# Two-layer hybrid block on one core: three of sixteen shared experts of the second layer placed between routed experts, the others given out by pieces

## The chip, the core and the metric

The kernel runs on one NeuronCore of a Trainium2 chip. The core has five engines with queues of their own: PE (TensorE, matrix products; the profile lists its weight loads apart, as PEld), DVE (VectorE), ACT (ScalarE), POOL (GpSimd) and SP (SyncE, which here only issues transfers). Each engine takes its instructions in the order in which the program gives them, and a waiting instruction holds what stands behind it on that engine. Transfers between HBM and the on-chip memory are issued from SP, ACT or POOL and are carried out by 16 DMA engines. The time is that of the whole program on the device, in microseconds (us); less is better.

## What is computed

16 sequences of 512 tokens with 256 features, 8192 tokens in all, all float32, pass four steps, each added to its input after a layer norm: attention with rotary positions, a mixture of experts, a linear attention with forget gates, and the same mixture of experts with the same weights again. The change lies in the mixture, which is:

```python
logits = x @ router_w.T                        # 64 experts
probs = softmax(logits)
topk_w, topk_ids = top_k(probs, 8)
topk_w = topk_w / sum(topk_w)
pos = cumsum(onehot)[token, expert] - 1        # place of a token in its expert
valid = pos < 128                              # an expert holds 128 tokens
h = silu(xb @ w_gate) * (xb @ w_up)            # per expert: 128x256 @ 256x192
y = h @ w_down                                 # 128x192 @ 192x256
routed = segment_sum(y[...] * topk_w * valid)  # back to the tokens
shared = silu(x @ ws_gate) * (x @ ws_up) @ ws_down   # every token
return routed + shared
```

The places are counted over all 8192 tokens in order, so an expert takes the first 128 tokens that chose it, and no expert can start before the last token's choice is known.

## The kernel before

Tokens are handled in 16 blocks of 512 (`BLK`), each 4 chunks of 128. `Block.attention` is the first layer, and it works off most of the first mixture's block work between its own steps; `Block.forget_attention` is the linear attention; `Block.routed` finishes a mixture, and with `loads=True` (the second layer) it does all of it. `Part` holds the state of one mixture: pools, weights, and a method for each step of a block. `Block.joined` closes the program.

All the order around the change is written out by hand: inside `tc.manual_schedule` the engines take their instructions in the order in which the code calls the steps.

The second mixture has three stages.

*Block loop* (`for b in range(-4, nb + 1)`, L1266). In one turn it loads block b+4 (`load`), chooses the experts of block b (`choose`, L1573), normalises block b+2 (`normed`), turns block b+1 for PE (`features`), runs the shared expert of block b-3 (`gu`, `silu`; `lag` is 3) and its down product for block b-4 (`down`), takes logits and exponentials of b+1 (`logits`, `likely`, `exps`), counts block b (`count`: turns on PE and a copy on ACT; `added`: a running sum, L1617, carried over from block to block), and takes the moments of block b+3. `choose` divides the exponentials by their sum (L1577 to L1579) before it takes the eight largest (L1587, L1588); the weights are divided by the sum of the eight afterwards. Normalised rows and weights are stored in the table `rows` (`rows<-xn`, `rows<-wt`), counts in the table `counts`, and `counted` reads them back into `cw` with chunks in the partitions (L1506) as soon as they are stored; the last block's counts go from chip memory to `cw` directly (`straight`, L1510, two rows on SP and two on ACT). The shared expert's result y is stored into `routed` on SP (L1691). In turns 2 to 6 one pair of experts' weights is fetched each (`fetch`, four pieces on SP).

*Tail.* `chunks_before` (L1069 to L1073) needs all counts. It copies the chunk totals and forms their running sum on PE. `find` then works out in five pieces which token stands in which place, for two or four experts at a time (`place` advances it), and `gather` fetches the 128 rows of an expert from `rows` (L1133, an indirect DMA on POOL). Between these calls stand the shared experts of the last two blocks and the last three down products.

*Routed experts* (`for e in range(done - 2, E)`). In turn e the kernel gathers expert e+6, advances a lookup, turns the rows of e+2 (`turned`), multiplies e+1 by gate and up (`widened`, L1163), multiplies e by down (`narrowed`, L1187), scales it on ACT into `ye` (L1195) and adds it to the tokens' rows by an indirect DMA on POOL (L1198). Even experts add into the output, odd ones into `routed`, so two accumulators take turns, and an addition waits for the one before into the same accumulator. Weights come in pairs of experts into 11 slots, fetched piece by piece on SP.

At the end `joined` adds `routed` to the output in eight DMAs on POOL (L1381).

Before the stages, `begin` (L1438) loads the router and the shared expert's weights on ACT's queue and stores zeros into the rows behind the last token.

Of the kernel before, what the change touches and what calls it, by code (L numbers as in the profile page):

```python
# [26 lines left out]
E = 64  # L27
# [10 lines left out]
class Block:  # L38
# [131 lines left out]
    def attention(self, x, x1, wqkv, wo, rope, part, later):  # L170
# [14 lines left out]
        with ExitStack() as c:  # L185
# [271 lines left out]
            def each(s):  # L457

                n, i = divmod(s, CB)
                yield groups, n, weighted, i  # L460
                yield groups, n + 2, largest, i
                b, at = divmod(s, steps)

                now = [
                    (self.nblk, b + far, work, *args)
                    for work, far, *args in dense[at]
                    if b + far < z - 2 or work not in expert
                ]
                if i == 0:
                    yield groups, n - 1, summed  # L470
                if i == 1:
                    yield groups, n + 3, turn, kTs, H, "kT"
                    yield from now[0:1]
                    yield groups, n - 1, heads
                    yield groups, n + 1, row
                    now = now[1:]
                if i == 2:
                    yield groups, n + 3, turn, qTs, 0, "qT"
                yield from now
# [542 lines left out]
    def routed(self, part, loads=False):  # L1022
# [9 lines left out]
        with ExitStack() as c:  # L1032
# [6 lines left out]
            if loads:  # L1039
                part.look_up("right")  # L1040
                part.slots(5, "right")
            else:
                part.slots(4, "right")
# [81 lines left out]
            accs = (x, y)  # L1125
# [56 lines left out]
            def narrowed(e):  # L1182
                wd = ws[e // 2][1]
                he = hidden[e % len(hidden)]
                py = bank()
                for m in range(2):
                    nc.tensor.matmul(  # L1187
                        py[:, 0:D],
                        lhsT=he[:, m, :],
                        rhs=wd[:, e % 2, m, :],  # L1190
                        start=(m == 0),
                        stop=(m == 1),
                    )
                ye = p8.tile([P, D], F32, name="ye")
                nc.scalar.activation(  # L1195
                    ye, py[:, 0:D], AF.Copy, scale=xes.pop(e)[:, D + e : D + e + 1]
                )
                nc.gpsimd.indirect_dma_start(  # L1198
                    out=accs[e % 2],
                    out_offset=bass.IndirectOffsetOnAxis(ap=token[:, e : e + 1], axis=0),  # L1200
                    in_=ye,
                    in_offset=None,
                    compute_op=ALU.add,
                )
# [5 lines left out]
            with tc.manual_schedule(  # L1210
# [8 lines left out]
                nb, lag, ahead = self.nblk, 3, 6  # L1219
# [33 lines left out]
                def counts(b):  # L1253
                    part.added(b, stored=b < nb - 1)
                    (part.counted if b < nb - 1 else part.straight)(b)

# [8 lines left out]
                if loads:  # L1265
                    for b in range(-4, nb + 1):  # L1266
# [6 lines left out]
                        run(b - lag, nb, gu)  # L1273
                        run(b - lag, nb, silu)
# [3 lines left out]
                        run(b, nb, counts)  # L1278
                        run(b - 1 - lag, nb, down)
                        run(b + 1, nb, part.exps)  # L1280
                        run(b + 3, nb, lambda b: part.moments(b, xs[b]))
                        if 2 <= b < 7:
                            fetch(b - 2)
                        if b == nb:
                            chunks_before()
                            place(0, 3)

                    begun, done, z = 5, 0, nb - 1
# [3 lines left out]
                    part.gu(z - 1, 0)  # L1292
                    place(2, 1)
                    part.gu(z - 1, 1)
                    place(2, 1)
                    gather_to(3)
                    silu(z - 1)
                    part.down(z - 2, 0)
                    part.down(z - 2, 2)
                    place(4, 3)  # L1300
                    part.gu(z, 0)
                    place(4, 1)
                    part.gu(z, 1)
                    place(4, 1)
                    gather_to(5)
                    silu(z)
                    down(z - 1)
                    down(z)
# [43 lines left out]
                part.own.close()  # L1352
                part.slots(part.pairs - len(part.slot), "left")

                rest = [(n, piece) for n in range(begun, E // 2) for piece in range(4)]
                due, last = len(rest), E - 10
                for e in range(done - 2, E):
                    if e + ahead > 5:
                        run(e + ahead, E, gather_to)
# [4 lines left out]
                    run(e, E, narrowed)  # L1364
                    while rest and (due - len(rest)) * last < due * (e + 1):
                        n, piece = rest[0]
                        if e < 2 * (n - part.pairs) + 3:
                            break
                        if piece == 0:
                            held(n)  # L1370
                        part.fetch(*rest.pop(0))
# [28 lines left out]
class Part:  # L1400
# [6 lines left out]
    def __init__(self, ctx, k, x, y, weights, room, pairs, side):  # L1407
        rw, self.w_gate, self.w_up, self.w_down, ws_gu, ws_down = weights
        self.ctx, self.pairs, self.slot, self.ws = ctx, pairs, [], {}
        self.k, self.nc, self.x, self.y, self.room = k, k.nc, x, y, room  # L1410
# [23 lines left out]
        self.end = 0.0  # L1434
# [3 lines left out]
    def begin(self, queue):  # L1438
        rw, ws_gu, ws_down = self.shared_weights
        nc, T, w = self.nc, self.k.T, self.pools[1]  # L1440
        self.rw_sb = w.tile([P, KD, E], F32, name="rw_sb")
        queue.dma_start(out=self.rw_sb, in_=rw.rearrange("(k p) f -> p k f", p=P))
# [13 lines left out]
        for i in range(self.room["hT"]):  # L1456
            hT = w.tile([P, 2, BLK], F32, name=f"hT{i}")
            nc.gpsimd.memset(hT[FT:P, 1, :], 0.0)
            self.hidden.append(hT)
        for z in (self.rows, self.x, self.y):  # L1460
            queue.dma_start(out=z[T : T + P, :], in_=self.k.zeros[:, 0 : z.shape[1]])

# [47 lines left out]
    def straight(self, b):  # L1510

        for i in range(CB):
            at, queue = b * CB + i, (self.nc.sync, self.nc.scalar)[i % 2]
            queue.dma_start(out=self.cw[at : at + 1], in_=self.cum[:, ts(i, P)])
# [58 lines left out]
    def choose(self, b, piece):  # L1573
        nc, small, pr = self.nc, self.k.small, self.prs[b]
        if piece == 0:
            sm = small.tile([P, CB], F32, name="sm")
            nc.vector.tensor_reduce(sm, pr, AX.X, ALU.add)  # L1577
            nc.vector.reciprocal(sm, sm)
            nc.vector.tensor_tensor(  # L1579
                pr, pr, sm.unsqueeze(2).to_broadcast([P, CB, E]), ALU.mult  # L1580
            )
# [62 lines left out]

    def silu(self, b, piece):
        if piece == 0:
            self.hTs[b] = self.hidden[b % len(self.hidden)]
# [7 lines left out]
    def gate(self, b):  # L1655
# [3 lines left out]
        self.hTs[b] = self.hidden[b % len(self.hidden)]  # L1659
# [15 lines left out]
    def down(self, b, i, pool=None):  # L1675
# [3 lines left out]
        py = self.bank()  # L1679
        for k in range(2):  # L1680
            for m in range(2):
                nc.tensor.matmul(  # L1682
# [6 lines left out]
        nc.scalar.copy(self.ys[b][:, i : i + 2, :], py.rearrange("p (c d) -> p c d", c=2))  # L1689
        if i > 0:  # L1690
            nc.sync.dma_start(  # L1691
                out=self.y[ts(b, BLK), :].rearrange("(c p) d -> p c d", p=P),
                in_=self.ys.pop(b),
            )
            del self.hTs[b]
# [3 lines left out]
def hybrid_block_kernel(  # L1699
# [29 lines left out]
    with ExitStack() as c:  # L1729
        part = Part(c, k, attended, routed, moe, ROOM, 13, "left")  # L1730
# [5 lines left out]
    with ExitStack() as c:  # L1736
        part = Part(c, k, out, routed, moe, ROOMY, 11, "left")
# [73 lines left out]
```

## Time and profile before

| | us |
|---|---|
| three runs | 2657.08, 2655.26, 2654.50 (median 2655.26) |
| the profiled execution, its own time | 2656.52 |
| span from its first to its last instruction | 2654.5 |
| mean granted TensorE clock | 0.951 of full speed |

| share of the span | busy us | instructions |
|---|---|---|
| PE | 2430.0 (92%) | 17864 |
| DVE | 1852.8 (70%) | 4677 |
| ACT | 1333.0 (50%) | 2750 |
| POOL | 843.2 (32%) | 835 |

The shares are means over stages of different kinds. The first attention takes the span to 1339 us with PE at 1320 busy; the first mixture's rest ends at about 1609, the linear attention at about 2128, and the second mixture and the closing sum fill the remaining 526 us. A line of the profile names the source line, the engine, the operation, what is written and read, and how often. In the chain of waits each piece is the work that ended last before the next could start; a timeline lists start, length and the idle time before an instruction with what ended it.

### The profile page before, as it was taken

The page shows a single profiled execution, that of the slowest core. Times are in us where ns is not written, and L with a number is a line of the kernel's source. Part 1 is how long each engine was busy: PE and PEld are TensorE (multiplying, and loading weights), DVE is VectorE, ACT ScalarE, POOL GpSimd, SP SyncE. Part 2 cuts the span into 40 slices and gives each one's busy share as a digit, 9 for nine tenths or more (in the row PEclk, how much of TensorE's full clock was granted, in tenths as well). Part 3 has the DMA queues.
Part 4 walks back from the last instruction along what each step waited for, and adds up shares of the span by engine and source line. Part 5 has one row for each costly group of instructions (what it writes and reads, how often), then busy time and mean ns, then how long its engine had stood idle before and what let it go on. Part 6 is the DMA issues. An engine that isn't in the chain of part 4 may idle for free.

```text
span 2654.5 us, 47730 instructions
## 1 busy us (share of the span) xinstructions
PE 2430.0 (92%) x17864; PEld 1512.9 (57%) x17864; DVE 1852.8 (70%) x4677; ACT 1333.0 (50%) x2750; POOL 843.2 (32%) x835
## 2 busy tenths in 40 slices
PE   7999999999999999999988886899999969998881
PEld 3444555455555554555446775577777646667671
DVE  6566777767777766776646664889889869967660
ACT  1566666666666666666542332466566513323330
POOL 3122212222221222112015776423223021127773
PEclk8899999999999999999888998999999969999996
DMA  1000111001110011100157987212111068749987
GB/s 57 1 10 27 35 37 35 14 29 35 37 35 16 27 37 35 37 27 6 57 123 223 235 223 164 80 34 65 49 57 49 25 149 191 169 113 263 245 212 148
DMA packets 210003, 226.47 MB, mean 85 GB/s; under 512 B 34286, under 2 KB 202222, under 8 KB 208750
## 3 DMA queue, kind: packets, MB, share of 16 engines
q1 hardware_dynamic: 180366, 174.43, 22.8%
q0 software_dynamic: 25728, 46.15, 8.8%
q8 instruction: 142, 2.33, 0.4%
q10 hardware_dynamic: 3680, 2.85, 0.3%
q14 instruction: 87, 0.71, 0.1%
HBM read 146.50 MB, written 84.48 MB: 87 GB/s over the span
## 4 chain that ended last, share of the span: by engine, by line
PE 76%; DVE 9%; DMA 9%; issue 2%; POOL 2%; ACT 1%; SPq 0%; ACTq 0%; POOLq 0%; DVEq 0%
PE sc L334 20%; PE sc L384 9%; DMA xe<-rows,token 5%; PE sc L260 4%; PE pb L809 4%; PE sc L1637 3%; PE sc L323 3%; PE sc L841 2%; PE sc L1682 2%; PE sc L1163 2%; PE pb L873 2%; PE sc L407 2%; PE sc L304 2%; PE pb L918 2%; PE pb L734 2%
## 5 line engine op out<-in xcount | busy, mean ns | idle before, releaser
L348 DVE TENSOR_REDUCE mx<-sc 128x1 f32<-128x512 f32 x1024 | 635.0, 682 | 293.8 <-PE sc L334 293.7
L374 ACT ACTIVATE pT<-sc 128x512 f32<-128x512 f32 x1024 | 527.8, 604 | 110.3 <-PE sc L334 110.3
L334 PE MATMUL sc<-qT,kT 17*128 17x512 f32 x2048 | 315.0, 647 | 0.0
L334 PE MATMUL sc<-kT,qT 16*128 16x512 f32 x2048 | 301.5, 609 | 0.3 <-DVE mx L348 0.3
L384 PE MATMUL sc<-pT,v 128*32 128x512 f32 x2048 | 243.7, 618 | 0.0
L104 POOL TENSOR_SCALAR va<-mv 128x4 f32<-128x4 f32 x64 | 14.6, 228 | 700.8 <-DVE mv L98 690.1
L858 DVE SCALAR_TENSOR_TENSOR pT<-sc,of,left 128x256 f32<-128x256 f32 x512 | 205.0, 474 | 20.2 <-PE sc L841 18.9
L334 PEld LDWEIGHTS sc<-kT,qT 16*128 16x128 f32 x2048 | 151.1, 190 | 91.9 <-issue 36.5
L282 POOL TENSOR_TENSOR t<-qk,rope_sb 128x512 f32<-128x512 f32 x62 | 78.6, 1267 | 382.2 <-ACT qk L268 374.6
L334 PEld LDWEIGHTS sc<-qT,kT 17*128 17x128 f32 x2048 | 94.3, 185 | 128.4 <-issue 95.3
L384 PEld LDWEIGHTS sc<-pT,v 128*32 128x32 f32 x2048 | 61.6, 113 | 174.2 <-issue 124.0
L1133 POOL DMA_INDIRECT xe<-rows,token x128 | 128.7, 1006 | 96.9 <-DVE token L1115 39.6
L260 PE MATMUL sc<-wqkv_sb,feat 128*128 128x512 f32 x256 | 124.8, 613 | 0.0
L144 ACT COPY oT<-sc 128x512 f32<-128x512 f32 x64 | 37.4, 585 | 172.7 <-PE sc L384 172.7
L809 PE MATMUL pb<-feat,wqk_sb 128*128 128x512 f32 x256 | 117.7, 593 | 0.0
L1198 POOL DMA_INDIRECT routed<-ye,token x64 | 102.9, 1608 | 41.7 <-DMA routed<-ye,token 9.6
L323 PEld LDWEIGHTS sc<-ident,pad 128*128 128x128 f32 x512 | 55.3, 144 | 104.2 <-ACT pT L374 81.9
L96 DVE BATCH_NORM_STATS2 bn<-x 128x6 f32<-128x256 f32 x256 | 89.1, 411 | 16.8 <-DMA x<-out 13.4
L1597 POOL TENSOR_TENSOR wt<-pr,chosen 128x256 f32<-128x256 f32 x32 | 23.2, 725 | 241.4 <-DVE chosen L1592 217.1
L323 PE MATMUL sc<-ident,pad 128*128 128x128 f32 x512 | 86.8, 293 | 5.1 <-POOL pad L298 2.8
L1637 PE MATMUL sc<-xnT,wsg_sb 128*128 128x512 f32 x192 | 90.9, 600 | 0.0
L290 POOL TENSOR_TENSOR t<-qk,rope_sb 128x256 f32<-128x256 f32 x124 | 90.6, 752 | 0.0
(225 smaller groups left out, 4900.3 us busy)
## 6 DMA issues: line engine op xcount, KB each, us to landing
ws<-in_w_gate SPq DMA_DIRECT2D x64, 384.0 KB
ws<-in_w_up SPq DMA_DIRECT2D x64, 384.0 KB
rows<-xn SPq DMA_DIRECT2D x32, 512.0 KB
routed<-y SPq DMA_DIRECT2D x32, 512.0 KB
ws<-in_w_down SPq DMA_DIRECT2D x64, 256.0 KB
x<-in_x SPq DMA_DIRECT2D x16, 512.0 KB
attended<-x SPq DMA_DIRECT2D x16, 512.0 KB
ws<-in_w_down SPq DMA_DIRECT2D x64, 128.0 KB
```

The source lines that it names most:

```text
L260: nc.tensor.matmul(pq, lhsT=xnTs[b][:, kd, ts(i, P)], rhs=wqkv_sb[:, kd, 0 : 2 * D], start=(kd == 0), stop=(kd == KD - 1),)
L290: eng.tensor_tensor(t2[:, :, lo : lo + HD // 2], qk2[:, :, :, 1 - half], rope_sb[:, i, HD + lo : HD + lo + HD // 2] .unsqueeze(1) .to_broa ...
L323: nc.tensor.transpose(pt[:, ts(i, P)], pads[b % 2][i][:, at : at + 4, :].rearrange("p h d -> p (h d)"), self.ident,)
L334: nc.tensor.matmul(scs[j], lhsT=lhs[at : at + high, ts(i, P)], rhs=rhs[at : at + high, :], start=True, stop=True,)
L348: nc.vector.tensor_reduce(mxs[n][:, j, i : i + 1], sc, AX.X, ALU.max, negate=True)
L374: nc.scalar.activation(pT[:, j, :], sc, AF.Exp, scale=float(HD) ** -0.5)
L384: nc.tensor.matmul(pav[ts(j, HP), :], lhsT=vs[b % 2][:, i, 4 * hg + j, :], rhs=pT[:, j, :], start=(i == 0), stop=(i == CB - 1),)
L809: nc.tensor.matmul(pq, lhsT=wqk_sb[:, kd, ts(m, P)], rhs=xnTs[b][:, kd, :], start=(kd == 0), stop=(kd == KD - 1),)
L858: nc.vector.scalar_tensor_tensor(pTs[n][:, :, ts(s8, HD)], sc[:, :, ts(s8, HD)], of[:, s8 : s8 + 1], here, ALU.mult, ALU.mult,)
L1133: nc.gpsimd.indirect_dma_start(out=xes[e], out_offset=None, in_=rows, in_offset=bass.IndirectOffsetOnAxis(ap=token[:, e : e + 1], axis=0),)
L1198: nc.gpsimd.indirect_dma_start(out=accs[e % 2], out_offset=bass.IndirectOffsetOnAxis(ap=token[:, e : e + 1], axis=0), in_=ye, in_offset=No ...
L1637: self.nc.tensor.matmul(to, lhsT=self.wsg_sb[:, kd, ts(m, P)], rhs=self.xnTs[b][:, kd, :], start=(kd == 0), stop=(kd == KD - 1),)
```

## The change

It does these things:

- `choose` no longer divides by the sum of the exponentials; this holds for both mixtures.
- Blocks 3, 7 and 11 of the second mixture are put off (`put_off`): their shared expert is left out of the block loop, and zeros are stored for them in `begin`. It runs between the routed experts in 24 pieces (`between`), with the shared weights loaded a second time and the normalised rows read back from `rows`; three DMAs on POOL add the results (`paid`).
- The other 13 blocks' shared experts are a list of pieces with costs, 130 units in all, of which each turn of the loop gives out its share up to 110; the last 20 go before and between the lookups.
- Counts are read back one block later (`counted` of b-1), `straight` issues all four rows on ACT, and y is stored on ACT's queue in the second mixture.
- Early weights are fetched as two pieces in every block from 3 on, in place of four in blocks 2 to 6. The second mixture has 9 slots of weights, not 11.
- The accumulators are taken in turn (`next(accs)`) whoever adds.

The core of the diff:

```diff
-            accs = (x, y)
+            accs = itertools.cycle((x, y))
...
-                    out=accs[e % 2],
+                    out=next(accs),
...
                 if loads:
-                    for b in range(-4, nb + 1):
+                    own = [b for b in range(nb) if b not in part.put_off]
...
+                    pieces = []
+                    for n, b in enumerate([*own, None]):
+                        if b is not None:
+                            pieces.append((4, b, first_part, b))
+                        if n > 0:
+                            pieces.append((2, own[n - 1], part.down, own[n - 1], 0))
+                            pieces.append((2, own[n - 1], part.down, own[n - 1], 2))
+                        if b is not None:
+                            pieces.append((2, b, second_part, b))
+                    total, spent = 10 * len(own), 0
...
+                    for b in range(-4, nb):
...
-                        run(b - lag, nb, gu)
-                        run(b - lag, nb, silu)
+                        shares((total - 20) * (b + 1) // nb, b)
...
-                        run(b, nb, counts)
-                        run(b - 1 - lag, nb, down)
+                        run(b, nb, lambda b: part.added(b, stored=b < nb - 1))
+                        if b == nb - 1:
+                            part.straight(b)
+                        run(b - 1, nb - 1, part.counted)
...
-                        if 2 <= b < 7:
-                            fetch(b - 2)
+                        for _ in range(2):
+                            if b >= 3 and early:
+                                part.fetch(*early.pop(0))
+                    shares(total - 10)
+                    chunks_before()
+                    place(0, 3)
+                    shares(total - 8)
                     place(0, 2)
                     gather_to(1)
                     place(2, 3)
+                    shares(total - 6)
+                    place(2, 2)
                     gather_to(3)
...
                 for e in range(done - 2, E):
+                    if open_piece:
+                        next(filler, None)
+                        open_piece = False
...
+                    if e >= 0 and begun_pieces * (E - 14) < all_pieces * (e + 1):
+                        next(filler, None)
+                        open_piece = begun_pieces % 8 > 0
+                        begun_pieces += 1
+                    if part.owed and e >= E - 12 and e % 3 == 0:
+                        part.paid(next(accs))
...
+        for b in self.put_off:
+            for i in range(CB):
+                at = b * BLK + i * P
+                queue.dma_start(out=self.y[at : at + P, :], in_=self.k.zeros[:, 0:D])
...
     def choose(self, b, piece):
         if piece == 0:
-            sm = small.tile([P, CB], F32, name="sm")
-            nc.vector.tensor_reduce(sm, pr, AX.X, ALU.add)
-            nc.vector.reciprocal(sm, sm)
-            nc.vector.tensor_tensor(
-                pr, pr, sm.unsqueeze(2).to_broadcast([P, CB, E]), ALU.mult
-            )
...
+    def between(self, side):
...
+        for b in self.put_off:
+            xn = pool.tile([P, CB, D], F32, name="xn_o")
+            nc.sync.dma_start(
+                out=xn, in_=self.rows[here, 0:D].rearrange("(p c) d -> p c d", c=CB)
+            )
+            yield
+            for kd in range(KD):
+                pt = self.bank()
+                for i in range(CB):
+                    nc.tensor.transpose(
+                        pt[:, ts(i, P)], xn[:, i, ts(kd, P)], self.k.ident
+                    )
+                yield
+                nc.scalar.copy(xnT[:, kd, :], pt)
+                yield
+            for m in (0, 2, 1):
+                gu = self.bank()
+                self.chunk(b, m, gu)
+                yield
...
+            for i in (0, 2):
+                py = self.bank()
+                self.lowered(py, hT, i)
+                yield
+                nc.scalar.copy(y[:, i : i + 2, :], py.rearrange("p (c d) -> p c d", c=2))
+                yield
+
+    def paid(self, to):
+        here, y = self.owed.pop(0)
+        self.nc.gpsimd.dma_start(
+            out=to[here, :].rearrange("(p c) d -> p c d", c=CB), in_=y, accum_op=ALU.add
+        )
...
-        part = Part(c, k, out, routed, moe, ROOMY, 11, "left")
+        part = Part(c, k, out, routed, moe, ROOMY, 9, "left", (3, 7, 11))
```

`chunk` is a gate or up product of a block (two float32 matmuls of 512 columns, which the profile lists as four rows) and `lowered` the down product of half a block (the four matmuls that `down` had before, eight rows). After each matmul piece the copy, tanh or SiLU that reads it stands at the start of the next expert's turn.

## The prediction

> **What bounds the kernel now.** The change reaches almost only the second expert layer, so I read the stretches first (start and end in us, length, busy us with instruction counts of PE, PEld, DVE, ACT and POOL, granted clock, DMA share, GB/s), cut where that layer changes character:
>
> ```profile
> 2142.40:2341.20 198.80, 179.31 (x795) 128.69 (x796) 182.22 (x628) 58.51 (x112) 41.67 (x64) 0.87 0.72 167
> 2341.20:2378.80 37.60, 34.63 (x122) 21.84 (x121) 18.55 (x40) 8.84 (x16) 6.14 (x6) 0.95 0.34 99
> 2378.80:2575.00 196.20, 166.24 (x1119) 146.00 (x1117) 129.33 (x362) 65.08 (x170) 140.77 (x112) 0.97 0.91 243
> 2575.00:2609.30 34.30, 21.93 (x146) 18.66 (x146) 10.94 (x31) 9.09 (x23) 22.53 (x18) 0.92 0.53 84
> 2609.30:2654.50 45.20, 0.00 (x0) 0.00 (x0) 0.00 (x0) 0.00 (x0) 6.80 (x8) 0.50 0.91 186
> ```
>
> The block loop is VectorE's (182.22 of 198.80 busy); the tail up to the first expert is TensorE's (34.63 of 37.60, DMA at 0.34); the experts use PE, POOL and DMA heavily together; the closing sum is DMA alone. The timeline of DVE in the loop shows what a block is made of (start us, us, engine, line):
>
> ```profile
> 2300.93 0.38 DVE L1577 TENSOR_REDUCE sm<-pr 128x4 f32<-128x256 f32 x1
> 2301.34 0.18 DVE L1578 RECIPROCAL sm<-sm 128x4 f32<-128x4 f32 x1
> 2301.55 0.42 DVE L1579 TENSOR_TENSOR pr<-pr,sm 128x256 f32<-128x256 f32 x1
> 2302.01 0.23 DVE L1587 MAX8 top<-pr 128x8 f32<-128x64 f32 x1
> ...
> 2307.11 0.67 DVE L1018 SCALAR_TENSOR_TENSOR th<-th,pb 128x512 f32<-128x512 f32 x1
> ...
> 2309.92 0.42 DVE L1564 TENSOR_REDUCE mx<-pb 128x4 f32<-128x256 f32 x1
> ```
>
> Nothing waits between them: scans (L1617) start at 2298.16 and 2310.72, 12.56 us a block. Normalising is 2302.01 - 2300.93 = 1.08 us of it, a shared expert's SiLU 2309.92 - 2307.11 = 2.81 us.
>
> The chain of waits shows the tail as shared experts (L1637 gate and up, L1682 down):
>
> ```profile
> 2354.29 5.33 PE pb L1637 x8
> 2359.61 0.64 PE pb L1095 x4
> 2360.25 1.91 PE pb L1637 x4
> 2362.17 3.45 PE pb L1682 x16
> 2365.62 3.43 PE pb L1637 x8
> ...
> 2372.05 6.91 PE pb L1682 x32
> ```
>
> So a block costs PE 5.15 (row 2332.67 of the same chain) + 3.46 = 8.6 us. For the experts, POOL's timeline:
>
> ```profile
> 2462.13 1.59 POOL L1198 DMA_INDIRECT routed<-ye,token  x1 [0.30 <-issue]
> 2464.03 0.99 POOL L1133 DMA_INDIRECT xe<-rows,token  x1 [0.30 <-issue]
> 2466.09 1.59 POOL L1198 DMA_INDIRECT out<-ye,token  x1 [1.08 <-DMA out<-ye,token]
> 2467.98 0.99 POOL L1133 DMA_INDIRECT xe<-rows,token  x1 [0.30 <-issue]
> 2469.27 1.59 POOL L1198 DMA_INDIRECT routed<-ye,token  x1 [0.30 <-ACT th L1172]
> ```
>
> A gather and a scatter-add cost 0.99 + 0.30 + 1.59 + 0.30 = 3.18 us, and POOL has little rest: 64 experts took 2596.7 - 2378.8 = 217.9 us, 3.40 each. PE's own need comes from the rows at 2561.67, where the turns of an expert start, and 2564.39, where the next lookup starts: 2.72, plus a quarter of a lookup's 1.09, 2.99 us. POOL leads, PE follows.
>
> **The change, part by part, to the profiled execution** (2656.52 us; span 2654.5, 2.0 around it).
>
> *Loop.* (a) Normalising goes, 16 x 1.08 = -17.3 us, all of it on DVE's path up to the last scan; the ratio of the weights is unchanged by it. (b) Before that scan 13 SiLUs ran; the new budget, 110 of 130 units, holds 12 first and 11 second halves, 11.5: -1.5 x 2.81 = -4.2. (c) Counts are read back a block later, y goes out on ACT's queue. The waits of SP's queue show
>
> ```profile
> SPq L1506 <- DMA counts<-cum: 56.6, 13, 6.7
> ```
>
> (total us, times, longest), with x loads and stores queued behind. But DVE lost only some 5 us to late transfers in the loop (from scan 2162.47 to scan 2339.92 177.5 us; blocks 9.67, 12.56 and the shorter last ones add up to 172.6). The bounds are -5 and +5 (y's issue on ACT, 0.41 us on SP, holds up the copies and tanh behind it when an older transfer is late); I take 0, because weights now come as two pieces in every block from 3 on and keep DMA as full as the 0.84 that I read for 2185 to 2230. (d) begin() gets 12 more stores of zeros, 1.5 MB, on ACT's queue just where the first x loads run; the same row's kind, 1.5 MB of x, took from 2138.3 to about 2145 there, so 0 to +6; +2, since DVE needs the second and third x only 5 and 10 us later. On ACT the first copy is at 2148.24, with 11 us of room against 12 x 0.4 us of issue. (e) The first shared expert starts at block 0 rather than 3. The granted clock was 0.50 until 2182 and 0.70 then 1.00 as L1637 began; 12 matmuls at half clock cost 5.15 more. 0 to +5; I take +2, nearer the lower end because the clock was already 0.70 over the first 3 us of them.
>
> The Trainium skill, "TensorE: Matmul & The Clock Gate", Part 1, says that about 3.4 us of sustained matmuls release the clock. The windows at 2182 to 2188 agree; by the rule (e) would be some 1.7 us, by the row of half clock 5.2.
>
> The Trainium skill, "DMA: Bandwidth & Descriptors", Rules for kernel authors, speaks against (c): other issuing queues share the same 16 engines, and only issue time is saved. By it (c) is 0; if SP's 56.6 us were all on the path it would be far more, which the 172.6 excludes.
>
> Loop: -17.3 - 4.2 + 2 + 2 = -17.5.
>
> *Counts to lookup.* From the last scan to L1069 took 2351.76 - 2339.92 = 11.8 us, because SP issued its two rows (L1514) only at 2347.5. All four on ACT: scan 1.3, issues 2.4 (1.19 for two), landing 3.0 (after 2348.7) to 6.4 (first layer, 1386.1 to 1392.5): 6.7 to 10.1. Ten units on PE beside it (8.6 us, then tanh 0.6 and DVE 1.4) end about 9 after the scan. I take 9: -2.8 (bounds -5, -1.7).
>
> *Tail.* From 2351.76 to 2378.80 is 27.0 us. Now 5 x 1.73 of shared work, lookups 0.68 + 0.64 + 1.09, the first product 0.6, and some 2 for the last tanh and SiLU: 13.6. The other path, tokens 4.0 + issue 1.4 + landing 4.5, is shorter. -13.4 (bounds -16, -9). The first expert starts 33.7 earlier.
>
> *Experts.* Three blocks return: 8 turns 0.87 (L1543 x8 in the chain) + 8.61 = 9.5 each, 28.4 us of PE, spread over experts 0 to 49: PE then needs 2.99 + 0.57 = 3.56 a piece, against 3.40 taken before, so +8; up to 28.4 if POOL loses all of it, 0 if it overlaps wholly. ACT gets 18 copies and tanh of 0.6 and DVE 12 operations of 0.7, in 65 and 129 busy of 196: hidden; without cover 11 and 8. A tanh or SiLU that waits for a piece holds ACT's ye and DVE's xeT behind it, POOL's scatter next. DMA: three xn of 0.5 MB, 0.58 MB of shared weights again, through SP ahead of weight fetches: 2.1 MB at 243 GB/s is 9 us in a stretch with 9% free, hence +1. The weights' two memsets on POOL replace two of six for slots (11 pairs become 9). Three sums of 0.5 MB are turns of the accumulators on POOL at experts 54, 57, 60: joined's rows give 0.85 to issue, 5.65 us per MB, so 1.15 + 2.8 = 4 each if scatters wait, 12; gathers end at 57 and DMA is 0.53 there, so +5. Together +14 (0 to +40).
>
> *Rest.* First layer: two more issues on ACT (0.56 and 0.85) ahead of tanh at 1386.13, in its chain: +1.4. Its removed normalising lies beside PE, at 1320 of 1339 busy, or ends 2 us before the count's turns: 0. Closing sum unchanged.
>
> Sum: -17.5 - 2.8 - 13.4 + 14 + 1.4 = -18.3, span 2636.2, execution 2638.2. The runs' median, 2655.26, is 1.3 below the profiled execution: **2637 us**.
>
> **Rivals.** *Expert stage pays everything* (slower). PE's order and POOL's 3.18 decide: a piece stands before the next turns, ye comes late, and POOL, with 0.22 us of rest an expert, never catches up. 28.4 + 12 = +40 in place of +14: 2663. For: 3.56 is above both 3.18 and 3.40. Against: 6 gathers ahead and 8 buffers of ye, and PE itself waited 27.8 us for xe. It decides from +38 on, 4.0 us an expert. *Loop bound elsewhere*: PE (43.0 of 45 busy from 2185) and DMA 0.84 keep the pace, (a) gains 4 only: 2637 + 13 = 2650. Against: PE's load falls from 11.6 (turns 0.87, logits 1.73, count 0.43, shared 8.6) to 8.9 us a block, DVE's to about 10.5. *All hidden*: PE's pieces fall into its waits, sums behind the last experts, +0: 2623.
>
> **How the numbers follow.** Forecast 0.50, all paid 0.20, loop elsewhere 0.14, all hidden 0.16. 0.2% (5.3 us) is about what a measurement tells from no change: faster than 2650 is the forecast, all hidden and 0.02 of the loop's case, 0.68; 0.12 of that case and 0.01 of all paid are within, 0.13; 0.19 slower. The range: down to -14 on the experts and -5 on transfers with some loss elsewhere, 2616; up to all paid, 2663.
>
> **What would show it.** After: scans 10.5 us apart with SiLU, no L1577 to L1579; last scan near 2322; first expert near 2345; experts 3.5 to 3.6 us each to 50, POOL idle waiting for ye; first joined near 2591. Wrong if DVE idles over 10 us in the loop for L1637 or x, if experts take 3.8 and more, or if scatters wait over 4 us after each sum.

## The result and the profile after

The changed kernel takes 2668.58 us (median of 11 runs, 2661.36 to 2673.47); the kernel before, run on the same chip, takes 2656.5 us (11 runs, 2650.64 to 2663.11). The ratio is 1.0036 with a 95% interval of 1.0024 to 1.0049: about 10 us slower, where 18 us less were forecast, and outside the range. The profiled execution after took 2668.04 us, span 2666.1, at a mean granted clock of 0.946.

Cut at the same marks in both traces (the last addition of the first mixture's experts on POOL; the last scan of the counts; the copy of the chunk totals; the first expert's turns on PE; the first DMA of the closing sum), the spans compare like this, in us:

| stretch | before | after | difference | predicted |
|---|---|---|---|---|
| start to the first mixture's last addition | 1644.9 | 1652.7 | +7.8 | +1.4 |
| from there to the last scan (linear attention, block loop) | 695.0 | 696.2 | +1.2 | -17.5 |
| last scan to the copy of the totals | 11.8 | 15.9 | +4.0 | -2.8 |
| copy of the totals to the first expert | 27.0 | 18.2 | -8.8 | -13.4 |
| experts | 230.5 | 237.6 | +7.1 | +14 |
| closing sum | 45.2 | 45.5 | +0.3 | 0 |

The first mixture's experts end at this mark, 1644.9 before, and not at the 1609 that the section on the time before gives. The first row is mostly scatter between executions: in the traces of the kernels below, whose first layers are nearly alike, this mark lies anywhere from 1641.9 to 1653.3. The second row is the one that counts. A loop that should have become 17.5 us shorter did not become shorter at all.

The stretches of the kernel after (start and end in us, length, busy us with instruction counts of PE, PEld, DVE, ACT and POOL, granted clock, DMA share, GB/s):

```profile
2153.20:2350.20 197.00, 169.47 (x765) 119.84 (x766) 163.39 (x574) 55.64 (x107) 41.73 (x64) 0.89 0.71 174
2350.20:2383.10 32.90, 21.51 (x68) 13.66 (x67) 14.63 (x35) 4.70 (x9) 5.53 (x5) 0.79 0.34 83
2383.10:2578.00 194.90, 186.10 (x1227) 161.75 (x1226) 136.90 (x374) 75.64 (x188) 142.35 (x113) 1.00 0.95 257
2578.00:2620.65 42.65, 22.82 (x146) 20.32 (x146) 10.96 (x31) 9.20 (x24) 27.02 (x20) 0.83 0.65 99
2620.65:2666.10 45.45, 0.00 (x0) 0.00 (x0) 0.00 (x0) 0.00 (x0) 6.83 (x8) 0.50 0.90 185
```

VectorE's work in the loop fell as foreseen, from 182.22 to 163.39 us. But the stretch is still 197 us long, so 17.0 of the 18.8 us that the work lost came back as idle time (33.6 us of it, where the kernel before has 16.6), while PE and the DMA engines are no fuller than before. Something that is none of these three holds the loop. VectorE's timeline shows what it waits for (in brackets the idle time and what ended it):

```profile
2275.45 1.27 DVE L1666 TENSOR_TENSOR_SCAN cum<-cs,cum 64x512 f32<-64x512 f32 x1
2282.07 1.40 DVE L97 BATCH_NORM_STATS2 bn<-x 128x6 f32<-128x256 f32 x4 [5.35 <-DMA x<-out]
...
2290.96 1.27 DVE L1666 TENSOR_TENSOR_SCAN cum<-cs,cum 64x512 f32<-64x512 f32 x1
```

These two scans are 15.5 us apart, and 5.35 of that is a block of x that came late. Up to block 13, blocks without a stall are 10.0 to 11.5 us apart, 10.7 on the mean, close to the predicted 10.5. In the waits of VectorE from 2160 to 2350 (total us, times, longest) x has the first place; the same wait took 3.0 us, once, in the kernel before:

```profile
DVE bn L97 <- DMA x<-out: 14.2, 5, 5.4
DVE mx L1618 <- PE pb L1606: 5.8, 3, 4.8
```

The second line belongs for the most part to the longest interval, 20.8 us before block 11, in which PE stalls too (e9 below). The chain of waits leads from x to its cause:

```profile
2243.86 0.59 ACT y L1733
2244.48 5.15 DMA routed<-y
2249.64 0.37 SPq L1548
...
2255.33 11.14 DMA x<-out
2266.50 1.41 DVE bn L97 x4
...
2277.56 3.47 PE pb L1745 x16
2281.05 0.59 ACT y L1733
2281.67 8.87 DMA routed<-y
2290.55 0.66 SPq L1548
2291.25 4.60 DMA x<-out
2295.88 1.40 DVE bn L97 x4
```

Read it upwards: VectorE waits for x, x was late because SP issued it late (and, the first time, because its transfer took 11.14 us, not 4.60), SP stood at a fetch of weights (L1548), and that fetch waited until a store of y, issued by ScalarE, had landed. The fetch has no data in common with y. SP's own timeline shows the hole:

```profile
2264.05 0.27 SPq L1560 DMA_DIRECT2D cw<-counts  x1
2274.75 0.38 SPq L1548 DMA_DIRECT2D ws<-in_w_gate  x1
2275.18 0.53 SPq L1548 DMA_DIRECT2D ws<-in_w_up  x1
2275.75 0.47 SPq L1062 DMA_DIRECT2D x<-out  x1
```

From 2264.32 to 2274.75 SP issued nothing, 10.4 us, and x is third in the line behind. The store it waited for is this one, in ScalarE's timeline:

```profile
2267.99 0.37 ACTq L1735 DMA_DIRECT2D routed<-y  x1
```

SP had reached the fetch 3.7 us before ScalarE even issued the store; in seven of its eight such waits SP stood before the store was issued. The waits of SP's queue over the loop and the tail (total us, times, longest) add up to 79.6 us of this:

```profile
SPq L1548 <- DMA routed<-y: 62.3, 6, 15.0
...
SPq L1650 <- DMA routed<-y: 8.8, 1, 8.8
SPq L1587 <- DMA routed<-y: 8.5, 1, 8.5
```

In the kernel before, SP's queue waited 0.2 us for y in this stretch, and 67.5 us for its own counts, which are now down to 2.3. One wait took the place of the other, and the new one is longer each time (up to 15.0 in place of 6.7). The records of the trace say why. Each transfer signals its landing by a completion semaphore, and in every trace of this case all transfers issued by SP and ScalarE share one ring of eight such semaphores; POOL's use eight others. The fetch of 2274.75 signals the same semaphore as the store of 2267.99 and waited for it before it was issued, and the seven transfers that SP had issued just before it carry the seven other semaphores. So in this program a transfer that would use a semaphore again waits until the earlier transfer on it has landed, whichever of the two engines issued that, and SP can run at most seven transfers ahead of a store that ScalarE has not issued.

The tail has the same queue in it. Its chain of waits after:

```profile
2348.94 1.29 DVE cum L1666
2350.25 9.06 DMA cw<-cum
2359.33 0.47 ACTq L1568
...
2364.82 0.22 DVE after L1072
...
2365.62 3.71 PE pb L1745 x8
2369.33 1.15 PE pb L1098 x4
2370.48 3.70 PE pb L1745 x8
...
2374.86 0.49 DVE near L1109
...
2378.41 1.16 PE pb L1098 x8
```

ScalarE's four issues of the last counts, in its timeline

```profile
2350.25 9.55 ACTq L1568 DMA_DIRECT2D cw<-cum  x4
```

took 9.5 us in place of the 2.4 that were booked: they start at 2350.25, 2350.84, 2354.45 and 2359.33, and the third and the fourth stood until an earlier transfer on their semaphore had landed. In addition PE, idle meanwhile, came back at half clock: 3.71 us for eight rows of L1745 that take 1.73 at full clock.

### The profile page after: what moved, and what is told of

The parts are those of the page before. It is cut to its first block, busy times and chain, and to the rows that moved or that the text cites. A ratio compares the mean times of both kernels' runs of the same rounds, so it can differ in the third digit from the quotient of the medians.

```text
span 2666.1 us, 47722 instructions
## 1 busy us (share of the span) xinstructions
PE 2435.6 (91%) x17888; PEld 1519.8 (57%) x17888; DVE 1820.6 (68%) x4581; ACT 1337.5 (50%) x2756; POOL 847.9 (32%) x838
## 4 chain that ended last, share of the span: by engine, by line
PE 78%; DVE 8%; DMA 7%; issue 2%; POOL 1%; ACT 1%; SPq 0%; ACTq 0%; POOLq 0%; DVEq 0%
PE sc L335 20%; PE sc L385 9%; PE sc L261 4%; PE pb L811 4%; PE sc L1686 3%; PE sc L324 3%; DMA xe<-rows,token 3%; PE sc L843 2%; PE sc L1745 2%; PE pb L1167 2%; PE pb L875 2%; PE sc L408 2%; PE sc L305 2%; PE pb L920 2%; PE pb L736 2%
## 5 line engine op out<-in xcount | busy, mean ns | idle before, releaser
L1686 PE MATMUL sc<-xnT,wsg_sb 128*128 128x512 f32 x192 | 90.9, 600 | 0.0
```

The lines of the kernel that those rows point to most:

```text
L1686: self.nc.tensor.matmul(to, lhsT=self.wsg_sb[:, kd, ts(m, P)], rhs=self.xnTs[b][:, kd, :], start=(kd == 0), stop=(kd == KD - 1),)
```

## The experiments

All times are medians of several runs against the kernel before on the same chip; differences in per cent and us are taken from the ratios. "After" is the changed kernel; where an edit starts from another version, it says so.

**y stored from SP again (e1).**

```diff
             if loads:
                 part.look_up("right")
                 part.slots(5, "right")
-                part.queue = nc.scalar
```

> The changed kernel with y stored on SP's queue again. In the changed kernel's trace SP's weight fetches, rows stores and x loads waited 80 us for y's stores (62.3 + 8.8 + 8.5), and DVE stood 25.3 us for x. Theory S (a transfer on SP waits for an earlier store that ACT issues late, and everything behind it on SP is late): DVE's wait for x falls below 10 us, first to last scan from 173.9 to some 155 us, the kernel 2668 -> about 2650. Rival D (the DMA engines are full in the loop, whoever issues): the same bytes move, the wait stays near 25 us, the time stays within 4 us of 2668.

2649.32 us, ratio 0.9961 [0.9946, 0.9976]. One line of the change thus costs 0.75%, 20 us, and without it the change is a gain. From the first mixture's last addition to the last scan it takes 680.7 us, 15.5 less than after, the scans are 10.0 to 11.7 us apart but for one (15.6) and the two shorter ones at the end, and neither SP waits for y nor VectorE for x in the loop. Another 2.7 us come from the counts in the tail: last scan to copy 13.2 against 15.9.

**y stored from POOL (e2).**

```diff
-                part.queue = nc.scalar
+                part.queue = nc.gpsimd
```

> The changed kernel with y stored on POOL's queue, neither ACT nor SP. Theory S: SP no longer waits for y at all, DVE's wait for x falls below 8 us, first to last scan some 152 us, the kernel about 2648; POOL has 12 of 15 us free in the loop and pays about 1 us a store. Rival D: as with SP, within 4 us of 2668. If the store's place in the order matters more than its queue, this run gains and the one with SP does not.

2652.63 us, 0.9972 [0.996, 0.9985]; the loop takes 681.9. So it isn't that y must be on SP to be in time. A third queue, outside the ring of semaphores, does nearly as well, and it is ScalarE's queue that does the harm.

**The store on ScalarE alone, put into the kernel before (e11).**

```diff
         if i > 0:
-            nc.sync.dma_start(
+            self.queue.dma_start(
...
-        self.end = 0.0
+        self.end, self.queue = 0.0, k.nc.sync
...
                 part.slots(5, "right")
+                part.queue = nc.scalar
```

> The kernel before, with y of the second mixture stored from ScalarE's queue and nothing else changed. Theory A (transfers issued on SP wait for stores issued on ScalarE, whatever else is done): the profile shows SP waiting some 20 to 80 us for routed<-y in the loop, x later at VectorE than before, last scan 3 to 15 us later counted from the first; ratio 1.002 to 1.006. Rival B (the store on ScalarE costs only together with the counts that are read back a block later, since in the kernel before SP waits for its counts in any case): waits for routed<-y under 15 us, ratio 0.998 to 1.001.

2676.96 us, 1.0067 [1.0043, 1.0091], 17.8 us slower (11 to 24 by the interval): theory A, above the upper end of what it expected. The lines of SP's waits:

```profile
SPq L1621 <- DMA routed<-y: 58.9, 7, 15.4
SPq L1507 <- DMA counts<-cum: 51.5, 15, 7.0
```

Four blocks are 17.0 to 18.9 us apart where the others are 12.6, and VectorE waits 20.8 us for x in the loop, 3.0 before. Here nothing else of the change is present, so the cost needs neither the new order nor the later read-back.

**Only the normalising removed, from the kernel before (e3).**

```diff
-            sm = small.tile([P, CB], F32, name="sm")
-            nc.vector.tensor_reduce(sm, pr, AX.X, ALU.add)
-            nc.vector.reciprocal(sm, sm)
-            nc.vector.tensor_tensor(
-                pr, pr, sm.unsqueeze(2).to_broadcast([P, CB, E]), ALU.mult
-            )
```

> The kernel before, with the three normalising instructions of choose taken out and nothing else. My prediction's term: 16 x 1.08 us on DVE's path in the loop, so 2656 -> about 2639, first to last scan from 177.5 to some 161 us. Rival D: DMA or PE keeps the pace, the loop shortens by 4 us or less and DVE's wait for transfers grows instead, the kernel about 2652.

2656.37 us, 0.9988 [0.9975, 1.0001]: some 3 us of the 17.3, between 0 and 7 us by the interval. Undisturbed blocks are 11.5 apart in place of 12.6, so the edit is worth its 1.1 us in them; but three blocks now take 15.8 to 16.9 where one took 15.6 before, SP waits for its counts 73.5 us, 67.5 before, and VectorE waits for x 14.0 us, 3.0 before. At the new pace SP's queue no longer brought x in time.

**The normalising back in, y on SP (e7, from e1).** The same lines with plus signs.

> The changed kernel with y on SP and the normalising put back. In the kernel before, taking it out gave only some 3 us, because waits for x grew from 3.0 to 13.8 us. If those waits came from counts read back at once and weights in bunches, they are gone here, DVE alone holds the loop, and the 16 x 1.08 = 17 us show: 2649 -> about 2665. If PE or DMA holds the loop even so, it costs under 8 us: below 2657.

2662.8 us, 1.0016 [1.0003, 1.003]; against e1 0.55%, 14.6 us. Eleven of the fifteen intervals between scans grow by 1.1 us. With a queue that keeps up, the same three instructions are worth nearly what was predicted, 14.6 for 17.3; on the kernel before they were worth 3.

**The counts read back in their own block, y on SP (e8, from e1).**

```diff
-                        run(b - 1, nb - 1, part.counted)
+                        run(b, nb - 1, part.counted)
```

> The changed kernel with y on SP and counts read back at once, as in the kernel before. SP waited 67.5 us there for counts to land. If that wait is what made x late, DVE's wait for x comes back (5 to 15 us beside the first) and the kernel is 6 to 15 us above 2649. If bunched weights were the cause, or DVE has room for it, it stays within 3 us of 2649, and the last read-back may gain or lose 2.

2666.32 us, 1.0031 [1.002, 1.0042]; against e1 0.70%, 18.6 us. VectorE waits for x 14.3 us again. SP's queue waits for its counts:

```profile
SPq L1558 <- DMA counts<-cum: 68.7, 15, 7.1
```

So the part of step (c) that was booked at nothing holds a gain of 18.6 us and a loss of 20 us.

**No block put off (e4, from after; e6, from e1).**

```diff
-        part = Part(c, k, out, routed, moe, ROOMY, 9, "left", (3, 7, 11))
+        part = Part(c, k, out, routed, moe, ROOMY, 9, "left", ())
```

> The changed kernel with no block put off: all 16 shared experts by pieces (160 units, 140 of them in the loop), no zeros, no pieces between experts, no three sums; 9 slots stay. By the traces the expert stage took 237.6 us against 230.5, so it should fall back by 7 to about 231; the loop gets 2.5 more shared experts in it, 7 us of DVE, and more waits of SP for y if theory S holds. Both together: between 2664 and 2680. If putting off itself were what costs (my second rival before the run, 28 us and more in the expert stage), it would end below 2655.

> The changed kernel with y on SP and no block put off. Putting off by itself: the expert stage should fall from 238 to some 228 (225.8 was seen with none put off), while the loop gets 2.5 shared experts more, 2.5 x 2.8 = 7 us of DVE, if DVE is what holds the loop. So between 2644 and 2650, near no difference from y on SP alone. If the loop is held by transfers, the three stores of y more cost over 7 and it ends above 2652; if the pieces between the experts cost more than the stage shows, below 2642.

e4: 2671.45 us, 1.0042 [1.0029, 1.0054], no different from after. e6: 2657.72 us, 0.9992 [0.9979, 1.0005], 8 us slower than e1 where 2644 to 2650 was expected: a miss. In the traces e6's loop takes 699.8 us against e1's 680.7, and its experts 229.5 against 238.0. With y on ScalarE the same trade is even: loop 707.0 against 696.2, experts 225.8 against 237.6. So with y on SP putting off pays 8 us here, but more than the 2.5 shared experts in the loop is behind it. Without blocks put off, the budget gives out a second half and a down product of the same block in turns 4, 5, 12 and 13. In just these turns PE waits for VectorE's SiLU, 3.96, 1.03, 5.23 and 1.85 us, and the scans stand 16.2, 13.8, 15.4 and 13.8 us apart where their undisturbed neighbours stand 11.5 or less. This is the stall that e9 takes out of turn 11; how much putting off is worth without it was not run.

**The counts of the block before read back first (e5, from e1).**

```diff
+                        run(b - 1, nb - 1, part.counted)
                         run(b, nb, lambda b: part.added(b, stored=b < nb - 1))
                         if b == nb - 1:
                             part.straight(b)
-                        run(b - 1, nb - 1, part.counted)
```

> The changed kernel with y on SP, and counted of the block before put ahead of the last block's added and straight. With y on SP the lookup waited for the read-back of block 14, which SP could issue only at 2337.33, after the last block's direct rows (5.0 + 6.9 us in the chain). If that order on SP is what is late, the way from the last scan to the copy of the totals falls from 13.2 to 8 to 9 us and the kernel is 4 to 5 us below the one with y on SP (2649). Rival: the direct rows on ACT (2.5 us of issue, 5 of landing) end no earlier than the read-back would: within 2 us of it.

2645.2 us, 0.9948 [0.993, 0.9965]; on the average 0.13% better than e1, 3.5 us where 4 to 5 were expected, with intervals that overlap. The chain of e1 in the tail shows what it aims at: SP issued the read-back of block 14's counts only after the last scan, at 2337.33.

```profile
2332.35 4.97 DMA cw<-cum
...
2337.33 6.85 DMA cw<-counts
...
2344.26 0.23 DVE after L1071
```

In e5 the read-back goes out at 2334.65, before its last scan at 2334.97, and the copy follows 10.0 us after the scan, 13.2 in e1.

**A down product never in the turn of its own second half (e9, from e5).** In e1, e5 and e7 one scan interval stays long, 15.6 to 18.2 us, at block 11. PE's timeline of e1 there:

```profile
2281.78 0.59 PE L1744 MATMUL pb<-wsd_sb,hT 128*128 128x256 f32 x2
2287.39 2.93 PE L1744 MATMUL pb<-wsd_sb,hT 128*128 128x256 f32 x6 [5.01 <-DVE hT L1021]
2290.11 2.45 PE L1605 MATMUL pb<-rw_sb,xnT 128*128 128x64 f32 x16
```

Turn 11 is the only one in which the budget gives out the second half of block 9, the first of block 10 and a down product of block 9. That product needs the SiLU of its own block, which stands behind all of VectorE's other work of this turn, and the next block's logits (L1605) stand behind the product.

```diff
+                        fresh = set()
                         while pieces and spent + pieces[0][0] <= upto and pieces[0][1] <= newest:
-                            cost, _, work, *args = pieces.pop(0)
+                            if newest < nb and pieces[0][2] == part.down and pieces[0][1] in fresh:
+                                break
+                            cost, of, work, *args = pieces.pop(0)
+                            if work is second_part:
+                                fresh.add(of)
```

> The version with y on SP and the counts of the block before read back first (ratio 0.9948) still has one scan interval of 17.1 us at block 11, where the others are 10 to 11.5. Theory: turn 11 is the only one that gives out a second half (block 9) and a down product of the same block, so PE stands waiting for that block's own SiLU, behind everything that VectorE has to do first, and then runs at half clock. With the down product held until turn 12 the interval falls to about 11, the other stages stay, and the time falls by about 5 us: ratio 0.993. Rival: the long interval comes from a late row of x or from the clock alone; then it stays above 15, the ratio is 0.995.

2635.46 us, 0.9916 [0.9893, 0.9939]. The interval at block 11 is 11.5 us. This version is 22 us faster than the kernel before and 1.2% faster than the change as made. Its loop takes 678.5 us, 16.5 less than before, where the prediction has 17.5. The interval shows that the stall is gone; the total doesn't resolve what it was worth, for the interval of the ratio overlaps that of e5, and e10, which keeps the stall (15.65 us), is as fast.

**The last counts on SP and ScalarE in turn (e10, from e5; e12, from e9).**

```diff
-            at = b * CB + i
-            self.nc.scalar.dma_start(out=self.cw[at : at + 1], in_=self.cum[:, ts(i, P)])
+            at, queue = b * CB + i, (self.nc.sync, self.nc.scalar)[i % 2]
+            queue.dma_start(out=self.cw[at : at + 1], in_=self.cum[:, ts(i, P)])
```

> The same version with the last block's four rows of counts on SP and ScalarE in turn again, as before the change, in both mixtures. Theory: in the first mixture ScalarE's two extra issues stand in the chain, some 1.2 to 2 us, which come back; in the second, SP has nothing late in front of its two rows once the counts of the block before are read back first, so last scan to copy of totals stays at 10 us or falls to 9. Ratio 0.994 (from 0.9948). Rival: SP's rows stand behind SP's store of y and its read-back as in the kernel before, the copy of totals comes 11.8 us or more after the last scan, and the ratio is 0.995 to 0.996.

> The down product held until the next turn (ratio 0.9916 by itself) and the last block's counts on SP and ScalarE in turn (0.992 against 0.9948 without, where 0.994 was expected) together: y on SP, the counts of the block before read back first. If the two gains are independent, the ratio is 0.9916 - 0.0028 = 0.989; if the gain of the two queues was only spread between chips, it stays at 0.9905 to 0.992, with the copy of totals 10.4 us after the last scan as in both.

e10: 2638.88 us, 0.992 [0.99, 0.994]; e12: 2636.37 us, 0.9921 [0.9907, 0.9935]. e10 came out below the 0.994 expected, which is the end of its interval, but e12 is no better than e9, so no gain of the two queues can be told: last scan to copy is 10.4 us in e10 and 10.2 in e12, 10.5 in e9. The 1.2 to 2 us that ScalarE's two extra issues should cost in the first mixture are not resolved by these runs.

## Why the prediction was wrong, step by step

**The step that failed is (c)**, the queue of y and the later read-back, put at 0 with bounds of -5 and +5. The store on ScalarE costs 17.8 us alone (e11) and 20 us inside the change (after against e1). Its upper bound was built from y's issue on ScalarE and what is queued behind it there. It was not asked what on SP might wait for y, since no data ties SP's transfers to it, and the rule on issuing queues that the prediction quotes there speaks of bandwidth and issue time, not of such a wait. The other half of (c), the read-back a block later, is not nothing either: e8 has all the rest of the change with y on SP, and its loop takes 696.9 us, no less than the 695.0 before. The prediction took 5 us of late transfers in the kernel before from a sum of 172.6; the undisturbed intervals add up to about 174, which leaves the 3 us for which VectorE waited for x. Either figure said only how well SP's waits were hidden at 12.6 us a block; at 11.5 they lie bare, as e3 shows. So the later read-back is what lets the loop have the gains of (a) and (b) at all, 18.6 us. The forecast's 0 for it was a silent assumption that SP keeps up at the new pace, which the read-back makes true. Of the 18.7 us by which the loop missed its forecast, 15.5 are the store's (after against e1), 2.2 are the stall of block 11 (e1 against e9) and 1.0 is left.

**(a) Normalising, -17.3.** Right in kind: 1.1 us a block in e7 against e1, 14.6 us in all. The forecast treats it as a term that stands by itself, and e3 shows that it doesn't: alone it is worth some 3 us.

**(b), (d), (e) and the rest of the loop.** Taken together with (a) and a harmless (c), the loop was to lose 17.5 us; with y on SP it lost 14.3 (e1) and with the stall of block 11 gone 16.5 (e9). That stall, 5.0 us of PE waiting in e1, was not foreseen: pieces were counted, and which piece stands before which was not followed turn by turn. The zeros (d) can't be seen: the first scan comes 522.3 us after the last addition in after and 522.7 in e4, which stores none. For (d) and (e) together +4 was booked. With the old start of the loop this way takes 517.5 (before), 520.0 (e3) and 520.5 us (e11), with the new one 520.5 (e7) to 524.6 (e9), 522.8 on the mean, so some 3 us are seen. The first shared expert now runs on PE ahead of the first count (5.57 us of L1686 for 12 rows at 2165.32), and with no trace of the zeros these 3 us are probably its; no run tests it alone.

**Counts to lookup, -2.8 with bounds -5 and -1.7; measured +4.0.** The 9 us that were forecast became 15.9. The two things missing are both queues: ScalarE's four issues took 9.5 us, since two of them waited for earlier transfers, and the read-back of block 14 was late. With y on SP and the read-back first it is 10.0 (e5) and 10.5 (e9), a gain of 1.3 to 1.9.

**Tail, -13.4 with bounds -16 and -9; measured -8.8.** 18.2 us in place of 13.6. The first three pieces of PE after the copy ran at half clock, 3.71 + 1.15 + 3.70 where 1.73 + 0.64 + 1.73 had been booked, 4.5 us; and 3.5 us of VectorE's own steps between two lookups (2374.86 to 2378.37) were left out, while the 2 us that were booked for tanh and SiLU, and one of the five pieces of shared work, lay beside other work. Even in e9 the stage takes 16.7.

**Experts, +14; measured +7.1.** The sum was too high, and wrong inside. Three blocks of work on PE were booked at +8, since PE would need 3.56 us an expert against 3.40. But 3.40 is a mean over all 64, with the last thirteen at 2.9. The first 50, where the pieces stand, took 3.63 us each before and 3.56 after. The same kernels without pieces took as long as those with them (3.56 in e4 and in after, 3.62 in e6 and in e1), so no cost of the 28.4 us of PE work can be seen; e5, at 3.72, shows the scatter. The last thirteen took 37.6 us before and 46.2 after (45.2 in e1, 46.1 in e9; 36.9 in e6 and 35.7 in e4, which have no sums). That is 8 to 10 us for the three sums, booked at 5 and bounded by 12. POOL's timeline after shows two of them:

```profile
2596.98 1.55 POOL L1813 DMA_DIRECT2D routed<-y_o  x1
2600.62 1.60 POOL L1202 DMA_INDIRECT out<-ye,token  x1 [2.09 <-ACT wc L1158]
...
2608.21 0.92 POOL L1813 DMA_DIRECT2D routed<-y_o  x1 [0.69 <-DMA routed<-ye,token]
2610.51 1.61 POOL L1202 DMA_INDIRECT out<-ye,token  x1 [1.38 <-DMA out<-ye,token]
2614.41 1.57 POOL L1202 DMA_INDIRECT routed<-ye,token  x1 [2.30 <-DMA out<-ye,token]
```

A sum takes POOL up to 1.6 us, not the 1.15 booked, and additions that followed each other 1.9 to 2.7 us apart at the end before are now up to 4.7 apart.

**The rivals.** "Expert stage pays everything" came closest in time (2663) and is wrong in its mechanism: the stage paid 7 us of the 40. "Loop bound elsewhere" had the right place and the wrong bound: PE (169.47 of 197 busy) and DMA (0.71) had room, SP's order of issue did not. "All hidden" was right for the pieces on PE and wrong for the sums. The list of things that would show the forecast wrong named the sign that appeared: VectorE idle in the loop for x.

Why the same wait does no harm while SP issues y itself can be read from e1's records. In the loop SP issues seven other transfers before it comes to the store's semaphore again, 10.7 us or more after the store; the stores of after landed 2.9 to 9.2 us after their issue. SP can't run ahead of a store that it issues itself, and by then the store has landed: SP doesn't wait for y in e1 at all. Open is the first row of the table: its 7.8 us lie within the 11 us by which that mark moves between executions.

## What to carry to other kernels

When a transfer is moved to another engine's queue, ask also which transfers of the *old* queue may wait for its landing through a shared completion semaphore, though no data connects them; a hole in one queue's timeline that ends with another queue's transfer is the sign, and such a ring is a risk where two engines that run at different paces share it. A wait that is hidden today is measured against today's pace: before an engine is made faster, price every wait at the new pace (e3: 3 us gained of 17). And compare a new need with the pace of the very stretch where the work will stand, not with the stage's mean.

## What the runs showed of the hardware that was not expected

In after the stores of 0.5 MB for which SP waited landed 2.9 to 9.2 us after their issue, so a queue that waits for one loses up to 15.0 us with the time that the store itself comes late.

A short pause of PE is followed by half clock. In e1 this is the 5.01 us wait at block 11, here with the stretches around it (columns as above):

```profile
2274.00:2282.00 8.00, 8.00 (x38) 4.92 (x37) 7.69 (x27) 3.23 (x7) 1.45 (x3) 1.00 0.93 246
2282.00:2287.00 5.00, 0.38 (x2) 0.00 (x0) 4.76 (x17) 0.00 (x0) 1.68 (x3) 0.74 0.90 270
2287.00:2290.00 3.00, 2.61 (x6) 2.17 (x7) 1.71 (x3) 0.00 (x0) 0.00 (x0) 0.50 0.52 151
2290.00:2293.00 3.00, 3.00 (x23) 2.91 (x23) 0.40 (x1) 0.59 (x1) 0.00 (x0) 0.79 0.98 240
2293.00:2296.00 3.00, 3.00 (x18) 2.55 (x17) 2.75 (x7) 2.23 (x5) 0.00 (x0) 1.00 0.82 248
```

The clock (third number from the end) falls to 0.50 within the pause and is back at 1.00 within 6 us of PE's resuming. By the trace's record of the clock, half clock lasted from 2284.45 to 2291.27: it began 2.1 us after PE's last product and ended 3.9 us after PE had resumed. The interval between the scans grew by less than the pause, to 15.6 us from the 11.5 of e9. In the tail of after, where PE stood for 9.7 us, half clock lasted from 2360.38 to 2374.03: it began 4.9 us after PE's last product and ended only 8.9 us after PE had resumed at 2365.18.

The Trainium skill, "TensorE: Matmul & The Clock Gate", Part 1, says that a window of about 3.4 us of idleness halves the clock and a window of about as much sustained work restores it, and that the windows run freely. The two lengths of half clock, 6.83 and 13.65 us, are two and four such windows, which agrees; the 8.9 us of work before the clock came back are more than one of them.
